# A cross-attention block on one core: another written order of the same operations, and earlier output stores

## The chip, the cores and the metric

The kernel runs on one core of a Trainium2 chip, in float32. The metric is the device time of one execution in microseconds; the median of three runs counts. The names are those of the profile: PE is TensorE (PEld its weight loads), DVE is VectorE, ACT is ScalarE, POOL is GpSimd, SP is SyncE, which issues all the DMAs here.

## The reference

One transformer block with cross-attention, four sequences of 256 tokens against 512 context rows, width 512, 16 heads of 32, an MLP of 2048:

```python
B, LQ, LK, D, H, HD, INNER = 4, 256, 512, 512, 16, 32, 2048
q = (layer_norm(x, ln1) @ q_w + q_b) -> heads
k, v = (ctx @ k_w + k_b), (ctx @ v_w + v_b) -> heads
attn = softmax(q @ k.T / sqrt(HD))
hidden = (attn @ v) @ cproj_w + cproj_b + x
y = gelu(layer_norm(hidden, ln2) @ fc_w + fc_b, approximate=True)
out = hidden + y @ proj_w + proj_b
```

## The kernel before, in words

The tokens are worked on in two groups, g = 0 and 1, each through the same stages. Context and tokens are loaded in quarters (`cq`), transposed on PE (`turn_c`, from an identity matrix, into the bank `ps_c`) and copied to SBUF (`c`). Then come the value, key and query projections (`v`, `k`, `q`), the attention units, the output projection (`o`), the second layer norm (`y`), the MLP's first matrix (`fc`) and its second (`proj`, whose products are called `pd`).

Each projection multiplies 2x2 blocks by seven products in place of eight (Strassen's scheme in Winograd's form; the two MLP matrices use it twice, 49 products for each half of `fc` and for each group of `proj`). That leaves less work to PE, and gives the other engines many elementwise sums: of weights (`vws`, `kws`, `fw`, `pw`), of operands (`y0i`, `z1t`, `z1i`) and of results. The function `quad` emits the seven products `P1` to `P7` of one block into PSUM banks `X`, `Y` and `W`, and behind each the sums that take it out (`t1`, `c11`, `c22` and so on). `P1` can be issued in two halves (`a`, `b`). `grown` runs `quad` seven times for the outer level. In the very last block, `pd14`, the product `P4` goes to a bank of its own, and the DVE sum `oz` takes it straight to the output tile. `P4`'s operand is `z1i4_4`, a sum of 1024 columns, which on POOL goes in two halves.

An attention unit is named by group, batch pair and head (`s113`, `av123`): `s` are the scores, in 32-row tiles of PE; then a multiplication by the mask, a maximum, a subtraction (`less`) and an exponential, spread over POOL, DVE and ACT; `ss` are the sums of the exponentials; `av` multiplies them with the values, in 32-column tiles of PE.

What sets the order is a string, `PROGRAM`. It holds every operation's name once, some with a letter for the engine (`:V` DVE, `:A` ACT, `:G` POOL); `Order.run` reads it and the operations are emitted in that order, so each engine, and SP for the DMAs, works through its own operations as the string has them. A waiting instruction holds up everything behind it on its engine. A second string, `PLACES`, gives each buffer its slot in SBUF or its bank in PSUM, so which earlier buffer has to be finished with first. In the trace a tile carries the name of one buffer of its slot, which is why a later product can show an operand under an earlier name.

`proj.ending` runs behind the outer products whose results are final. It transposes the finished column blocks (`tr`, on DVE), adds the residual (`out`, on DVE or POOL) and stores the result in 32-column pieces (`so`). For group 1 and the first half of the rows (I = 0) this happens twice, for L = 0 behind `pd12` or for L = 1 behind `pd13`; behind the last outer product, `pd14`, the remaining quarter is turned on PE (`turn_o`), the residual is added (`ot`), and the stores `st1`, `st00` and `st01` end the kernel.

Of the kernel before, what the change touches and what calls it, by code (L numbers as in the profile page):

```python
# [16 lines left out]
P = 128  # L17
# [109 lines left out]
v0_0_t2:V fw0_00_0 xt0_6 c0_30:A v0_1_P6 c0t4:V fw0_00_1 v0_0_P2 kws2:G fw0i1_1:G v0_1_t2:V v0_0_c11 fw0i1_2:V v0_0_P5
v0_1_P2 fw0i1_3:V fw0i1_4:V rows8 rows2 fw0_11_1 v0_1_P5 v0_1_t3:A fw0_10_1 fw0s3:V rows3 rows5 mk~1 fw0i4_1:G
fw0i7_3:V v0_0_t3:A rows1 fw0i7_1:G xt0_4 v0_1_c11 kw01 vws4:V fw0_11_0 fw0i7_2:V xt0_2 stats_x0_30 qw10 fw0i7_4:G
stats_x0_20 k0_0_P7 fw1_11_1 cols fw0_01_0 cols~1 xt0_3 aggr_x0_20 fw0s1:V fw0s2:V xt0_0 qw11 xt0_1 k0_1_P2 fw0i5_1:G  # L130
fw0_01_1 k0_0_P2 stats_x0_21 k0_1_t1:A vws3:G k0_1_P6 k0_1_t2:A fw0i4_2:G xt0_7 fcd0_1_True aggr_x0_21 stats_x0_00
stats_x0_01 k0_1_c11 fw0i4_4:V fw0i5_2:G fw0i5_4:G stats_x0_11 v0_0_P3 aggr_x0_30 k0_0_t1:A fw1_01_1 stats_x0_10
aggr_x0_10 k0_0_P6 fw0i5_3:V aggr_x0_11 aggr_x0_00 fw0i6_1:G fw1_00_1 aggr_x0_01 k0_1_P5 kws4:G v0_0_c12:A eps_x0_0
k0_0_t2:A k0_1_t3:A fw0i6_2:V k0_0_P5 pow_x0_0 fw1_00_0 stats_x0_31 fcd0_7_True nb_x0_0 k0_0_t3:A eps_x0_1 fw1_11_0
fw0i6_3:V fcd0_5_False k0_1_P7 fcd0_7_False pow_x0_1 qw00 norm_x0_01:A k0_1_P3 fw0i2_1:V cb1_03 nb_x0_1 fcd0_5_True
fw1_01_0 norm_x0_10:A fcd0_6_False v0_1_P3 k0_0_c22 qw01 fw0i6_4:G fw0i2_3:G eps_x0_2 norm_x0_11:A v0_1_c12:A
aggr_x0_31 norm_x0_00:V k0_0_c11 turn_x0_00 turn_x0_20 pow_x0_2 fw0i4_3:V k0_1_c12:A k0_1_c22 qws1:V fw1i1_1:V
fcd0_6_True nb_x0_2 fw0i2_2:G fw0i2_4:G fw0s4:V k0_0_P3 x0_20:A eps_x0_3 pow_x0_3 x0_00:V xt1_2 fw1i1_3:G cb1_01
fw1_10_1 nb_x0_3 norm_x0_31:V qws2:V norm_x0_20:A fw1i2_1:G fw0i3_3:V k0_0_c12:A fw1i1_2:V k0_1_P4 cb1_12 fw1i4_1:G
fw1i4_2:V turn_x0_30 fcd0_3_False turn_x0_10 fw1i2_2:V vd0_0_11 cb1_10 x0_10:A x0_30:A k0_0_P4 norm_x0_30:A q0_0_P1  # L140
norm_x0_21:A fw1i1_4:V k0_0_c21 fcd1_1_True q0_0_t1:A fw1i2_3:V k0_1_c21 q0_0_P2 q0_0_c11 fw1_10_0 fw1i2_4:G
turn_x0_01 x0_01:A fw1i4_4:G turn_x0_11 turn_x0_21 fcd1_2_True kd0_0_22 x0_11:V turn_x0_31 x0_31:A x0_21:A x0t1:V
x0t2:V q0_1_P1 q0_1_P2 s000 fw0i3_1:G qws3:V q0_0_P6 q0_0_t2:A ev000_11 x0t3:V fw0i3_2:G x0t4:V q0_1_t1:A fw1s1:V
fw1s2:V ev000_00 fw0i3_4:G fw1i4_3:G fcd1_4_True stats_x1_10 fw1i5_1:G fw1i5_2:G ev000_10 ev000_31 ev000_21 fw1s4:V
fw1i3_1:G q0_0_P7 q0_0_P5 q0_0_t3:A q0_0_c22 cb1_11 cb1_00 q0_1_P6 ev000_30 fw1i3_3:G cb1_02 kd0_0_11 q0_0_P4 ev000_01
kd0_0_21 fw1i3_2:G q0_1_t2:A q0_1_P5 mx000_0 ev000_20 mx000_1 q0_0_c21 mt000 q0_1_c11 mc000_3 fcd0_3_True xt1_3
fw1i5_4:G mc000_2 mc000_1 fold000 stats_x1_11 aggr_x1_10 fw1i3_4:G cT1_00 fcd1_5_False kd0_1_21 fcd1_6_False
aggr_x1_11 s020 ev020_00 ev020_10 q0_1_P7 qws4:G ev020_11 ev020_01 eps_x1_1 fcd0_2_True fw1s3:G q0_0_P3 ev020_30
fw1i6_1:V v0_0_P7 cb1_13 pow_x1_1 ev020_31 mx020_0 fcd1_3_False ev020_20 ev020_21 q0_0_c12:A md000 mx020_1 fw1i5_3:G
fw1i7_3:G mt020 nb_x1_1 cT1_01 fw1i7_1:G fw1i7_2:G q0_1_t3:A mc020_3 mc020_1 mc020_2 s002 fcd1_3_True cb1_32 ev002_11  # L150
ev002_31 fold020 fw1i6_3:G ev002_10 ev002_30 cT1_11 q0_1_P3 cT1_10 norm_x1_11:A fcd1_7_False fw1i6_2:G ev002_21
v0_1_P7 v0_0_c22 fw1i7_4:G ev002_20 ev002_01 ev002_00 mm000 md020 fw1i6_4:G fcd1_5_True q0_1_c12:V s022 ev022_11
ev022_01 ev022_00 v0_0_P4 ev022_10 cb1_33 q0_1_c22 ev022_20 ev022_30 ev022_21 q0_1_P4 c1t1:G ev022_31 s010 v0_1_c22
# [1354 lines left out]
```

## Time and profile before

| | |
|---|---|
| three runs, us | 652.28 (median), 652.1, 653.53 |
| the profiled execution, us | 652.72 |
| its span | 650.9 us |
| PE busy | 643.7 us, 99% of the span |
| DVE, ACT, POOL busy | 574.4, 346.0, 424.3 us |
| share of the chain that ended last, by PE | 88% |
| mean DMA rate | 222 GB/s |

The span runs from the first to the last instruction of the profiled execution; the 1.8 us between it and the execution's time lie outside the trace. A group row of the profile gives line, engine, operation, output and inputs, count, then busy us, mean ns of one, and the idle time just ahead of them with what ended it.

### The profile page before, as it was taken

To read this page: it belongs to the slowest core of one execution; us is meant where nothing else is said; L and a number is where in the kernel's file an instruction comes from. 1 tells how busy PE (TensorE), PEld (TensorE's weight loads), DVE (VectorE), ACT (ScalarE), POOL (GpSimd) and SP (SyncE) were. 2 spreads that over 40 slices of the span, in tenths; PEclk is the share of its full clock that TensorE was granted. 3 is DMA by queue.
4 is the path that set the end of the run, shared out by engine and by line. 5 is a ranking of instruction groups with operands and counts; after the bars stand their busy time and mean duration, and the time that the engine had idled before them with its cause. 6 is when DMAs were issued, how large, how long until landed. Compare 5 with 4: busy or idle time off the path is not lost.

```text
span 650.9 us, 11260 instructions
## 1 busy us (share of the span) xinstructions
PE 643.7 (99%) x3793; PEld 486.1 (75%) x3793; DVE 574.4 (88%) x970; ACT 346.0 (53%) x710; POOL 424.3 (65%) x377
## 2 busy tenths in 40 slices
PE   9999999999999999999999999999999999999997
PEld 7755464577445776777778888888888888888887
DVE  3998899999999999999999999999867778897684
ACT  2154689899999989976775547120220133621000
POOL 2573998888887996698959455222674536717563
PEclk9999999999999999999999999999999999999999
DMA  8999897778545459976768587979979598568855
GB/s 281 287 371 311 263 248 238 266 194 157 188 162 185 150 176 293 307 249 206 230 212 275 176 289 228 331 258 148 260 210 203 180 213 201 158 153 255 178 109 101
DMA packets 206585, 144.83 MB, mean 222 GB/s; under 512 B 117008, under 2 KB 166976, under 8 KB 206528
## 3 DMA queue, kind: packets, MB, share of 16 engines
q1 hardware_dynamic: 206528, 144.11, 77.7%
q8 instruction: 30, 0.49, 0.3%
q14 instruction: 27, 0.22, 0.1%
HBM read 104.10 MB, written 39.98 MB: 221 GB/s over the span
## 4 chain that ended last, share of the span: by engine, by line
PE 88%; DVE 6%; ACT 2%; DMA 2%; issue 1%; SPq 0%; DVEq 0%; ACTq 0%
PE pd_X L633 15%; PE fc_X L633 15%; PE fc_W L633 7%; PE pd_W L633 7%; PE av L633 6%; PE k_X L633 4%; PE s L633 4%; PE v_X L633 4%; PE pd_Y L633 4%; PE fc_Y L633 3%; PE o_X L633 3%; PE q_X L633 2%; PE k_W L633 2%; PE o_W L633 2%; PE v_W L633 2%; DVE mx L1032 2%
## 5 line engine op out<-in xcount | busy, mean ns | idle before, releaser
L613 ACT ACTIVATE pr<-s,cols 128x256 f32<-128x256 f32 x256 | 103.4, 484 | 11.6 <-PE s L633 7.4
L1056 POOL TENSOR_TENSOR pr<-pr,mm 128x512 f32<-128x512 f32 x76 | 100.1, 1348 | 2.8 <-DMA mm<-md 2.5
L1032 DVE TRANSPOSE_TENSOR_REDUCE mx<-pr 128x32 f32<-128x1024 f32 x64 | 76.7, 1218 | 2.1 <-ACT pr L613 1.9
L1236 ACT ACTIVATE h<-h,cols 128x256 f32<-128x256 f32 x128 | 54.7, 500 | 43.3 <-DVE h L624 24.5
L1059 ACT ACTIVATE pr<-pr 128x1024 f32<-128x1024 f32 x64 | 66.8, 1067 | 16.9 <-DVE pr L1052 8.3
L624 DVE TENSOR_TENSOR h<-fc_X,h 128x512 f32<-128x512 f32 x80 | 52.8, 675 | 7.2 <-PE fc_X L633 6.2
L624 DVE TENSOR_TENSOR h<-fc_W,h 128x512 f32<-128x512 f32 x48 | 31.8, 676 | 2.7 <-PE fc_W L633 2.3
L1052 DVE TENSOR_TENSOR pr<-pr,mm 128x1024 f32<-128x1024 f32 x26 | 33.4, 1303 | 0.0
L624 POOL TENSOR_TENSOR ss<-pr 128x512 f32<-128x512 f32 x19 | 25.6, 1357 | 10.8 <-ACT pr L1059 8.1
L1039 ACT COPY mx<-mx 32x64 f32<-32x64 f32 x96 | 23.3, 243 | 12.5 <-issue 5.8
L633 PE MATMUL pd_W<-z0i,pl 128*128 128x256 f32 x104 | 24.4, 379 | 0.0
L605 ACT ACTIVATE e<-pd_X,cols 128x256 f32<-128x256 f32 x4 | 1.9, 469 | 39.5 <-PE pd_X L633 26.0
L633 PEld LDWEIGHTS pd_W<-z0i,pl 128*128 128x128 f32 x104 | 19.8, 190 | 2.7
L624 DVE TENSOR_TENSOR po<-pd_X,po 128x256 f32<-128x256 f32 x24 | 9.9, 418 | 12.5 <-PE pd_X L633 12.5
L633 PE MATMUL pd_X<-z1i,pl 128*128 128x256 f32 x88 | 20.8, 379 | 0.0
L1040 DVE TENSOR_REDUCE mx<-mx 32x32 f32<-32x256 f32 x32 | 18.5, 579 | 2.6 <-ACT mx L1039 2.1
L624 POOL TENSOR_TENSOR tq<-tq,rq 128x512 f32<-128x512 f32 x8 | 10.1, 1266 | 16.2 <-DMA rq<-hd 11.6
L633 PE MATMUL fc_W<-y1i,fl 128*128 128x256 f32 x76 | 19.2, 380 | 0.0
L633 PE MATMUL pd_X<-z0i,pl 128*128 128x256 f32 x80 | 18.9, 379 | 0.0
L633 PEld LDWEIGHTS pd_X<-z1i,pl 128*128 128x128 f32 x88 | 16.7, 190 | 2.3
L624 POOL TENSOR_TENSOR h<-h,e 128x512 f32<-128x512 f32 x11 | 14.6, 1348 | 5.7 <-DVE e L624 5.7
L624 DVE TENSOR_TENSOR h<-fc_Y,h 128x512 f32<-128x512 f32 x24 | 16.1, 673 | 2.6 <-PE fc_Y L633 2.5
(603 smaller groups left out, 1865.8 us busy)
## 6 DMA issues: line engine op xcount, KB each, us to landing
mm<-md SPq DMA_DIRECT2D x32, 512.0 KB, 4.2
pl<-prd SPq DMA_DIRECT2D x56, 256.0 KB, 4.1
fl<-fcd SPq DMA_DIRECT2D x40, 256.0 KB, 3.5
fw<-in_L_xattn_fc_w_dram SPq DMA_DIRECT2D x16, 256.0 KB, 4.6
pw<-in_L_xattn_proj_w_dram SPq DMA_DIRECT2D x32, 128.0 KB, 3.0
hid<-in_x_dram SPq DMA_DIRECT2D x8, 512.0 KB, 3.9
hd<-hid SPq DMA_DIRECT2D x8, 512.0 KB, 5.7
fcd<-fw0i SPq DMA_DIRECT2D x7, 512.0 KB, 3.0
```

The costliest lines, as they stand in the source:

```text
L605: nc.scalar.activation(to(), of_(), AF.Identity, bias=bias(), scale=1.0)
L613: lambda e: nc.scalar.activation(to(), of_(), AF.Identity, bias=bias(), scale=1.0))
L624: E[e].tensor_tensor(to(), in0(), in1(), op)
L633: nc.tensor.matmul(o(), l(), r(), start=first, stop=True, skip_group_check=True)
L1032: T.op(f"mx{u}_{h}", [("DVE", 1.126)], [(pr[h], None)], [(mx, [h])], lambda e, h=h: nc.vector.tensor_reduce(tile_of(mx)[:, 0:64].rearrange ...
L1039: lambda e, a=a: nc.scalar.copy(tile_of(mx)[0:32, 64 + 64 * a : 128 + 64 * a], tile_of(mx)[32 * a : 32 * a + 32, 64:128]))
L1040: T.op(f"fold{u}", [("DVE", 0.38)], [(mx, [2, 3, 4, 5])], [(mx, [6])], lambda e: nc.vector.tensor_reduce(tile_of(mx)[0:32, 320:352], tile_ ...
L1052: nc.vector.tensor_tensor(p_, p_, m_[:, None, :].to_broadcast([P, 2, 512]), ALU.subtract)
L1056: E[e].tensor_tensor(p_, p_, m_, ALU.subtract)
L1059: lambda e, h=h: nc.scalar.activation(tile_of(pr[h]), tile_of(pr[h]), AF.Exp), table="exp")
L1236: lambda e, f=f, b=b, c=c: nc.scalar.activation(at(h[f][b], c), at(h[f][b], c), AF.Gelu_apprx_tanh, bias=col(c_fcb + f * 4 + c), scale=1.0 ...
```

## The change

Three things change. `PROGRAM` is replaced by another order of the same operations: 2999 names in place of 2991, with other engine letters at 123 elementwise operations. `PLACES` is replaced by another assignment of slots and banks. And in `proj.ending`, for group 1 and I = 0, each half of a column block is stored as soon as its own `out` is done, in sixteen stores of 64 KB in place of eight of 128 KB. The number of matmuls and of elementwise operations stays the same. Behind the tables all lines move down by two.

```diff
 PROGRAM = """
-cq0_00_0 vw00 cq0_00_1 turn_c0_10_0 turn_c0_00_0 c0_00_0:V c0_10_0:A small v0_0_P1a cq0_01_1 cq0_01_0 turn_c0_10_1
+cq0_00_0 turn_c0_10_0 turn_c0_00_0 vw00 c0_10_0:A c0_00_0:V small v0_0_P1a cq0_00_1 cq0_01_0 turn_c0_00_1 c0_00_1:V
...
 PLACES = """
...
-                if last:
+                if g == 1 and I == 0:
+                    for a in range(4):
+                        store(f"so{g}_{c}{a}_{L}", None, None, [(tq[c], [2 * L, 2 * L + 1])],
+                              lambda c=c, a=a: o_[512 * L : 512 * L + 512, c * P + 32 * a : c * P + 32 * a + 32].rearrange("(t i) j -> i t j", i=32),
+                              lambda c=c, a=a: tile_of(tq[c])[32 * a : 32 * a + 32, 512 * L : 512 * L + 512].rearrange("p (t j) -> p t j", j=32), 0.165)
+                elif last:
                     for a in range(4):
                         store(f"so{g}_{c}{a}", None, None, [(tq[c], [2 * x + y for x in part for y in range(2)])], lambda c=c, a=a: view[c][1](o_, a),
...
```

Three places of the new order follow. In a row stand the line, the operation, output and inputs with the number of the buffer behind the name, the shape, and how many such instructions follow each other.

At the start of the kernel, PE's instructions from the first value product on, in before. `v0_0_X` and `v0_1_X` are the banks of the first two value products, and the `ps_c` rows are transposes of the context quarters:

```order
L633 MATMUL v0_0_X_222<-vw00_206,c0_00_215 128x256 x2
L721 MATMUL ps_c0_10_1_228<-ident_64,cq0_00_204 128x128 x2
L721 MATMUL ps_c0_00_1_231<-ident_64,cq0_00_204 128x128 x2
L633 MATMUL v0_0_X_222<-vw00_206,c0_00_215 128x256 x2
L721 MATMUL ps_c0_11_247<-ident_64,cq0_01_225 128x128 x4
L721 MATMUL ps_c0_01_255<-ident_64,cq0_01_225 128x128 x4
L633 MATMUL v0_1_X_264<-vw00_206,c0_00_215 128x256 x4
```

The same stretch of PE in after:

```order
L635 MATMUL v0_0_X_221<-vw00_212,c0_00_214 128x256 x2
L723 MATMUL ps_c0_00_1_227<-ident_64,cq0_00_204 128x128 x2
L723 MATMUL ps_c0_10_1_231<-ident_64,cq0_00_204 128x128 x2
L635 MATMUL v0_0_X_221<-vw00_212,c0_00_214 128x256 x2
L635 MATMUL v0_1_X_239<-vw00_212,c0_00_214 128x256 x2
L723 MATMUL ps_c0_01_244<-ident_64,cq0_01_225 128x128 x4
L723 MATMUL ps_c0_11_252<-ident_64,cq0_01_225 128x128 x4
L635 MATMUL v0_1_X_239<-vw00_212,c0_00_214 128x256 x2
```

The first half of the second product now stands ahead of the transposes of the second quarter (`cq0_01`), the other half behind them.

In the attention units' last part, PE between two products of `fc015`, in before (`av123` and `s113` are two units' tiled matmuls, the others full-array products):

```order
L633 MATMUL fc015_X_3426<-y0t1_3084,fl015_0_3372 128x256 x2
L633 MATMUL av123_3432<-ss123_3366,ones_89 32x256 x4
L633 MATMUL av123_3432<-pr123_0_3135,vws1_297 32x256 x2
L633 MATMUL av123_3432<-pr123_1_3126,vws1_297 32x256 x2
L633 MATMUL av123_3432<-pr123_0_3135,vws1_297 32x256 x2
L633 MATMUL av123_3432<-pr123_1_3126,vws1_297 32x256 x2
L633 MATMUL fc015_Y_3453<-y0t1_3084,fl015_0_3372 128x256 x2
L633 MATMUL fc015_X_3426<-y0i5_3368,xn_x1_11_859 128x256 x2
L633 MATMUL s113_0_3464<-q1_1_12_2165,kw00_239 128x256
```

The same place in after:

```order
L635 MATMUL fc015_Y_3429<-y0t1_3017,v1_1_12_1657 128x256 x2
L635 MATMUL fc015_X_3408<-y0i5_3367,k1_0_11_998 128x256 x2
L635 MATMUL av123_3441<-ss123_3383,ones_89 32x256 x4
L635 MATMUL av123_3441<-pr123_0_3117,kw11_350 32x256 x2
L635 MATMUL av123_3441<-pr123_1_3148,kw11_350 32x256 x2
L635 MATMUL av123_3441<-pr123_0_3117,kw11_350 32x256 x2
L635 MATMUL av123_3441<-pr123_1_3148,kw11_350 32x256 x2
L635 MATMUL s113_0_3461<-kw11_350,xt0_5_444 128x256
```

`fc015_Y` (its `P2`) and the next `fc015_X` (its `P6`) no longer stand between the two units: `s113` follows `av123` directly, so one change from full-array to tiled matmuls falls away.

POOL's last operations in before (`tq` are the `out` sums, `po` the sums of finished blocks, `z1i4_4` the operand of the last product):

```order
L622 TENSOR_TENSOR z1i2_4_5733<-h1_30_4856,z1i2_2_5640 128x512 x2
L622 TENSOR_TENSOR z1i4_3_5755<-z1t4_3_5653,z1t4_1_5599 128x512 x2
L624 TENSOR_TENSOR po1_0_5205<-po1_0_5205,e1_5390 128x256
L624 TENSOR_TENSOR po1_1_5311<-po1_1_5311,e1_5390 128x256 x2
L624 TENSOR_TENSOR tq1_1_5775<-tq1_1_5775,rq1_1_5628 128x512
L622 TENSOR_TENSOR z1i4_4_5816<-z1t4_2_5729,z1i4_2_5694 128x512 x2
```

The same in after:

```order
L624 TENSOR_TENSOR z1t4_3_5714<-h1_31_4870,z1t2_3_5413 128x512 x2
L626 TENSOR_TENSOR tq1_0_5695<-tq1_0_5695,rq1_0_5311 128x512
L624 TENSOR_TENSOR z1i4_2_5731<-z1t4_3_5714,z1i4_1_5726 128x512 x2
L624 TENSOR_TENSOR z1i4_3_5781<-z1t4_3_5714,z1t4_1_5698 128x512 x2
L626 TENSOR_TENSOR po1_1_5354<-po1_1_5354,e1_5411 128x256
L626 TENSOR_TENSOR tq1_0_5695<-tq1_0_5695,rq1_0_5311 128x512
L626 TENSOR_TENSOR tq1_1_5648<-tq1_1_5648,rq1_1_5433 128x512
L624 TENSOR_TENSOR z1i4_4_5832<-z1t4_2_5611,z1i4_2_5731 128x512 x2
```

`out1_00` and `out1_10` (the two `tq` rows ahead of the last) now stand right ahead of `z1i4_4`; before, one such sum stood there, and it was another, `out1_11`.

More of the change, by code (lines that the diff above doesn't have):

```diff
@@ L127 @@
[L127 to L131, printed above, removed]
```

663 lines of the change are left out of this document (335 added, 328 removed).

## The prediction

> **What bounds the kernel now.** I read the page's engine shares first, then the chain that ended last, then a table of stretches, then the tensor engine's list of waits. Of the page these are the span, the busy times and the chain's shares by engine:
>
> ```profile
> span 650.9 us, 11260 instructions
> PE 643.7 (99%) x3793; PEld 486.1 (75%) x3793; DVE 574.4 (88%) x970; ACT 346.0 (53%) x710; POOL 424.3 (65%) x377
> PE 88%; DVE 6%; ACT 2%; DMA 2%; issue 1%; SPq 0%; DVEq 0%; ACTq 0%
> ```
>
> PE is busy for 643.7 of 650.9 us and carries 88% of the chain, and it has the same 3793 matmuls to do after the change. So the change can help only where PE waits, where PE changes between kinds of matmul, and at the two ends; it can hurt wherever another engine comes to be late for PE. The stretches below (length, then busy us and count for PE, its weight loads, DVE, ACT, POOL, then granted clock, DMA share, GB/s) show where that could be:
>
> ```profile
> core 0: us, PE busy (x) PEld busy (x) DVE busy (x) ACT busy (x) POOL busy (x), PEclk, DMA share, GB/s
> 0.00:25.00 25.00, 23.41 (x130) 19.19 (x131) 13.45 (x22) 4.37 (x7) 9.84 (x16) 1.00 0.88 268
> 25.00:50.00 25.00, 25.00 (x77) 13.45 (x76) 23.07 (x49) 11.03 (x17) 17.66 (x20) 1.00 1.06 351
> 50.00:75.00 25.00, 25.00 (x104) 12.50 (x103) 20.92 (x30) 12.99 (x26) 14.77 (x16) 1.00 0.97 298
> 75.00:100.00 25.00, 25.00 (x149) 14.43 (x148) 23.58 (x39) 21.48 (x52) 23.00 (x23) 1.00 0.98 253
> 425.00:450.00 25.00, 25.00 (x118) 22.00 (x117) 23.39 (x29) 3.51 (x5) 7.15 (x4) 1.00 0.84 224
> 625.00:651.00 26.00, 22.65 (x117) 19.94 (x115) 15.60 (x33) 0.00 (x0) 11.66 (x11) 1.00 0.53 97
> ```
>
> The clock is full everywhere, so it drops out. The first and last stretches are the only ones where PE is short of its 25 us by more than a little. The list of PE's waits (engine, line waited for, total us, times, longest) says how much could be won between them:
>
> ```profile
> PE ps_c L721 <- DMA cq<-in_ctx_dram: 0.6, 1, 0.6
> PE av L633 <- DVE ss L624: 0.5, 1, 0.5
> PE q_X L633 <- ACT q L605: 0.5, 1, 0.5
> PE o_W L633 <- DVE hid L624: 0.4, 1, 0.4
> PE q_X L633 <- ACT k L605: 0.4, 1, 0.4
> PE s L633 <- DVE q L624: 0.3, 1, 0.3
> PE fc_X L633 <- ACT xn_x L600: 0.2, 1, 0.2
> ```
>
> The first row lies at the start (below). The other six sum to 2.3 us in the whole middle of the kernel. That is small: nearly 3000 operations are reordered, and at most 2.3 us of waiting is there to be removed.
>
> **The start.** PE's first groups (start, length, the waiting time before it in brackets):
>
> ```profile
> 6.50 1.03 PE L633 MATMUL v_X<-vw,c 128*128 128x256 f32 x4
> 8.13 1.06 PE L721 MATMUL ps_c<-ident,cq 128*128 128x128 f32 x8 [0.60 <-DMA cq<-in_ctx_dram]
> 9.03 1.89 PE L633 MATMUL v_X<-vw,c 128*128 128x256 f32 x8
> 10.76 1.04 PE L721 MATMUL ps_c<-ident,cq 128*128 128x128 f32 x8
> ```
>
> Eight records of a value product take 10.76−9.03 = 1.73 us, so one is 0.216 us, and the group at 6.50 is over at 6.50+4×0.216 = 7.36. (The list's 0.60 reckons with a modelled end; start to start the gap is 8.13−7.36 = 0.77.) The change puts the first half of the next value product, four such records or 0.86 us, ahead of the two transposes that wait for that load. It needs only a quarter that has already been turned, and both copies of it, now on DVE, are out by about the time at which it starts. 0.86 covers 0.77, so I take the whole −0.77. Bounds: 0, if the later loads set the pace of the next products in any case, to −0.77. I take the upper end because the next transposes, at 10.76, start without any wait behind the product ahead of them; how much earlier than that their load lands, these rows don't say.
>
> **Changes of matmul kind.** The scores and the attention-times-value products use 32-row or 32-column tiles of PE. The order now joins some of these blocks: 36 separate visits stand between the full-array products, where 39 stood. One visit in before, with the products around it:
>
> ```profile
> 115.24 1.88 PE L633 MATMUL k_W<-c1t,kws 128*128 128x512 f32 x4
> 116.96 1.88 PE L633 MATMUL k_Y<-c,xt 128*128 128x512 f32 x4
> 118.77 0.64 PE L633 MATMUL av<-ss,ones 128*32 128x256 f32 x8
> 119.22 1.05 PE L633 MATMUL av<-pr,xt 128*32 128x256 f32 x16
> 120.20 1.98 PE L633 MATMUL k_X<-c,k 128*128 128x512 f32 x4
> 122.02 1.88 PE L633 MATMUL k_W<-c1t,vw 128*128 128x512 f32 x4
> ```
>
> A full product takes 116.96−115.24 = 1.72. k_Y is thus over at 118.68, and the visit starts at 118.77: 0.09 to enter. The product behind the visit takes 122.02−120.20 = 1.82: 0.10 more than the plain one. A visit costs 0.19 by these, and three fewer give −0.57, taken as −0.6. I do not count the cost of leaving the tiled matmuls, since where two blocks are joined they change between rows and columns inside the block instead. Bounds: 0, if PE had to wait there for an operand in any case, to −0.9 with some 0.1 each for leaving too.
>
> **The waits in the middle.** The same PE work stands ahead of every one of the six waiting products as before, so no new cover is put there, and what they wait for goes through the same engines. The one that the change touches is `av012`: the subtraction ahead of its exponentials goes from POOL to DVE, but its two sums of exponentials go from DVE to POOL. I take −0.3 for all six together. Bounds: −2.3 (all gone) to several us more (the second rival).
>
> **Engines.** 65 of the elementwise operations go from POOL to DVE (35 of 256 columns, 12 of 512, 18 of 1024), 60 from DVE to POOL (26, 19, 15), 20 from ACT to DVE and 18 from DVE to ACT. The rows that price them (DVE for 512, 1024, 256 columns, then POOL's two halves of a 1024-wide one with operands from elsewhere or from POOL itself):
>
> ```profile
> L624 DVE TENSOR_TENSOR h<-fc_X,h 128x512 f32<-128x512 f32 x80 | 52.8, 675 | 7.2 <-PE fc_X L633 6.2
> L624 DVE TENSOR_TENSOR z1t<-h,z1t 128x1024 f32<-128x1024 f32 x7 | 8.7, 1257 | 0.0
> L624 DVE TENSOR_TENSOR po<-pd_X,po 128x256 f32<-128x256 f32 x24 | 9.9, 418 | 12.5 <-PE pd_X L633 12.5
> L622 POOL TENSOR_TENSOR z1i<-h,z1i 128x512 f32<-128x512 f32 x8 | 12.6, 1586 | 6.9 <-DVE z1i L624 5.9 <-DMA out_dram<-tq 0.8 <-ACT h L1236 0.2
> L622 POOL TENSOR_TENSOR z1i<-z1t,z1i 128x512 f32<-128x512 f32 x10 | 12.4, 1269 | 1.4 <-issue 1.4
> ```
>
> Net, DVE gets 9×0.418 − 7×0.675 + 3×1.257 from POOL and two more of 0.675 from ACT: 3.76 − 4.73 + 3.77 + 1.35 = +4.2 us on 574.4. I cost it at nothing. Its cover is DVE's idle time: 1.93 + 4.08 + 1.42 = 7.4 us in the three stretches from 25 to 100 us, by the table, and the lead that the vector engine's results have over the product that reads them. The uneven part is early. Of the sums of MLP weights a net twelve 256-wide ones, one of 1024 and two of 512 come to DVE before about 110 us, and one of 512 leaves: 12×0.418 + 1.257 + 0.675 = 6.9 us, just under those 7.4. If that cover fails, it is the second rival. From about 376 us on PE does not wait at all (the stretch from 425 shows 25.00 of 25.00 with DVE at 23.39), and the order of products against their operands is no tighter there than before, so I count nothing.
>
> **The end.** The last PE groups, POOL's and DVE's last operations, and the stores (the last row: count, issue time min/median/max, first and last start):
>
> ```profile
> 643.02 1.89 PE L633 MATMUL pd_X<-z1t,pl 128*128 128x256 f32 x8
> 644.75 1.12 PE L1321 MATMUL ps_o<-ident,po 128*128 128x128 f32 x8
> 645.70 1.95 PE L633 MATMUL pd_V<-pl,z1i 128*128 128x128 f32 x16
> 641.13 1.27 POOL L624 TENSOR_TENSOR tq<-tq,rq 128x512 f32<-128x512 f32 x1 [4.63 <-issue]
> 642.36 2.50 POOL L622 TENSOR_TENSOR z1i<-z1t,z1i 128x512 f32<-128x512 f32 x2
> 647.69 0.42 DVE L624 TENSOR_TENSOR ot<-pd_V,ot 128x256 f32<-128x256 f32 x1 [0.89 <-PE pd_V L633]
> L593 SPq DMA_DIRECT2D out_dram<-tq x32: 315/506/1105, 525.2 to 644.1; - x32
> ```
>
> The last product, at 645.70, reads the sum `z1i4_4`, which POOL ends at 644.86: 0.84 early. In the new order POOL does `out1_10` right ahead of it, and `out1_10` needs results of the last but one block, `pd12`. From the end of that block's fourth product to the last product PE has three products and four transposes: 3×1.73 + 0.95 = 6.1 us. On the other side stand one sum (0.42), a transpose of about the same length, another sum and transpose, then 1.27 and 2.50 on POOL: 4×0.42 + 3.77 = 5.45, and by estimate a tenth for each of four or five handovers between engines (the nearest row is the 0.09 that PE took to enter a visit): 5.8 to 6.0. The 0.84 of slack shrinks to 0.1 or 0.3, and I take +0.1 since so little can be gone. Bounds: 0 to +0.8, the latter if POOL works at its slower row (1.586 for each of the three in place of 1.26, which makes the chain about 6.9).
>
> The eight last stores become sixteen of half the size. Ten go out behind the last two sums, and at 506 ns each SP is through with them at about the last product's start; the final store waits for DVE's 647.69 in any case. I take 0, hidden beside the last product and the sum behind it; uncovered it is up to 3×0.506 = +1.5. [...]
>
> **The sum.** −0.77 − 0.6 − 0.3 + 0.1 = −1.6 us, on a profiled execution of 652.72, which is 0.44 above the median of 652.28 and 1.8 longer than its span. Against the median: 650.7.
>
> **Rivals.** First, no change that can be told: the first and second terms hold, but waits grow elsewhere by about as much. The clearest place is POOL before the last product: at 1.586 for each operation the chain is 6.9 against PE's 6.1, +0.8 in place of +0.1, which gives −0.9 or 651.4. For it speaks that both paces stand in the profile for the same kind of operation, and that POOL gets one more late output sum; against it, that the very operations in question show the quick pace (the rows at 641.13 and 642.36). With new waits of under a microsecond at some of the attention products it is 651.4 to 652.3. [...]
>
> Second, slower: the 6.9 us of early weight sums are not absorbed by DVE. Its 7.4 us of idle are then not free time but waits for PE and for the loads (the DMA share is 0.97 to 1.06 there), and the lateness is carried on into the attention products, of which PE reads every result. Against it: those sums are wanted only by the MLP hundreds of microseconds later, and each is a word in a written order that can stand in a gap. Wholly unabsorbed it gives 652.3 − 1.6 + 6.9 = 657.6; half, 654.1. It decides from 1.6 + 1.3 = 2.9 us unabsorbed.
>
> Third, more than forecast: the 2.3 us of mid waits all vanish, because results come earlier through the new choice of engines: 650.7 − 2.0 = 648.7. For it speaks that fewer products now have their last operand's producer written close ahead of them (146 before, 129 now, with less than nothing to spare by the rows' durations); against it, the six places are the same.
>
> **How the numbers follow.** The forecast itself (650 to 651) has 0.38, the third 0.10, the first 0.32, the second 0.20. Measurements of this kernel can tell about 0.2%, 1.3 us, from no change; the first rival's time lies within that (over 651.0), the forecast and the third below it, the second above 653.6. So faster 0.48, same 0.32, slower 0.20. The range reaches down to 648.4 (the third, a little below it) and up to 654.6 (somewhat over half of the second), and leaves out some 0.06 below and 0.1 above.
>
> **What would show it.** The start: the wait for `cq` gone, and the 10.76 group 0.8 us earlier. The visits: 36, each still 0.2. The middle: PE's list of waits between 1 and 3 us. DVE: about 578 us busy, PE full from 25 to 75 us. The end: `z1i4_4` over within 0.3 us of the last product's start, and every half store landed before the final store. I am wrong if PE shows several short waits between 75 and 376 us that sum to over 2 us (the second rival), or if the loads after the first five land later than before.

## The result, and the profile after

The changed kernel is slower. Twenty executions of it have a median of 659.6 us (657.0 to 662.82), twenty of the kernel before on the same chip 657.41; the ratio of the comparison is 1.0078, with a 95% interval of 1.0056 to 1.0099. The forecast was 650.7 and a gain. One thing is needed to read these numbers: the kernel before has groups of times (651 to 655, 656 to 661 and 662 to 665 us), the ratio leaves the uppermost out, and the three times ahead of the prediction all came from the lowest; the first experiment tells why.

Three facts ahead of the prediction are to be put right: the inputs are eight sequences of 256 tokens, each against 256 context rows, and what is spread over POOL and DVE in an attention unit is the subtraction of the maximum, `less` (the `pr<-pr,mm` rows), while the mask is a bias that is added as the scores are copied out of PSUM. And 163 elementwise operations have another engine letter, not 123: the 65, 60, 20 and 18 of the prediction. None of the three enters the sum.

The page of the changed kernel, in the same three parts:

```profile
span 658.8 us, 11274 instructions
PE 647.1 (98%) x3793; PEld 487.1 (74%) x3793; DVE 579.9 (88%) x977; ACT 344.9 (52%) x708; POOL 411.4 (62%) x369
PE 66%; DVE 14%; ACT 7%; DMA 3%; POOL 3%; issue 3%; SPq 2%; DVEq 0%; ACTq 0%; POOLq 0%
```

PE has the same 3793 matmuls, but only 66% of the chain that ended last, where it had 88; DVE has 14 in place of 6. The span is 7.9 us longer: PE is idle for 4.5 us more, and busy for 3.4 us more with the same matmuls. Of these 3.4, some are slower first products, and some may be short waits, since the profile models the ends of matmuls (eight records that follow each other every 1.73 us are 1.89 us long in it). The stretches say where, first the changed kernel's, then two of the kernel before that were not shown:

```profile
core 0: us, PE busy (x) PEld busy (x) DVE busy (x) ACT busy (x) POOL busy (x), PEclk, DMA share, GB/s
0.00:25.00 25.00, 23.98 (x127) 19.25 (x128) 12.55 (x23) 6.33 (x11) 5.39 (x12) 1.00 0.81 247
50.00:75.00 25.00, 25.00 (x101) 12.26 (x100) 23.27 (x36) 11.88 (x25) 10.72 (x13) 1.00 1.01 301
200.00:225.00 25.00, 23.05 (x214) 15.64 (x207) 24.43 (x39) 22.66 (x51) 20.50 (x14) 1.00 0.33 115
375.00:400.00 25.00, 23.48 (x122) 18.67 (x121) 24.31 (x32) 13.80 (x34) 15.38 (x12) 1.00 0.52 174
```

```profile
200.00:225.00 25.00, 24.68 (x231) 16.95 (x228) 24.69 (x41) 23.86 (x55) 22.53 (x17) 1.00 0.52 171
375.00:400.00 25.00, 25.00 (x117) 21.84 (x116) 24.86 (x41) 12.76 (x31) 14.62 (x12) 1.00 0.76 245
```

From 25 to 75 us, where more weight sums came to DVE, PE is full. The largest losses lie at 200 to 225 and at 375 to 400 us, 1.6 and 1.5 us, where DVE is no busier than before. (Another 1.5 us is lost from 475 to 525 us, in the trace with late loads.) PE's list of waits in the changed kernel (engine, line waited for, total, times, longest):

```profile
PE s L635 <- DVE v L626: 1.9, 1, 1.9
PE fc_X L635 <- DMA fl<-fcd: 1.0, 2, 0.8
PE o_X L635 <- DVE a1t L626: 1.0, 1, 1.0
...
PE av L635 <- ACT pr L1061: 0.5, 1, 0.5
PE fc_W L635 <- DMA fl<-in_L_xattn_fc_w_dram: 0.5, 1, 0.5
PE fc_W L635 <- DVE h L626: 0.5, 1, 0.5
```

Between the start and the end there are seven waits of 0.5 us or more (1.9, 1.0, 0.8 and four of 0.5), where the kernel before had two. Most are of two kinds, late DVE results and loads of MLP weights (`fl`). The longest is `s110` at 216 us. DVE's rows just ahead of it, then POOL's, then PE's (start, length, and the wait in brackets):

```profile
210.11 0.40 DVE L626 TENSOR_TENSOR pw0i<-pw0i,pw 128x256 f32<-128x256 f32 x1
210.44 1.49 DVE L626 TENSOR_TENSOR pw0i<-pw 128x256 f32<-128x256 f32 x1
211.85 1.50 DVE L626 TENSOR_TENSOR pw0i<-pw,pw0i 128x256 f32<-128x256 f32 x1
213.27 2.29 DVE L1054 TENSOR_TENSOR pr<-pr,mm 128x1024 f32<-128x1024 f32 x1
215.49 0.68 DVE L626 TENSOR_TENSOR v<-q_Y,v 128x512 f32<-128x512 f32 x1
```

```profile
210.16 1.49 POOL L624 TENSOR_TENSOR a0t<-att,a0t 128x512 f32<-128x512 f32 x1 [0.36 <-POOL a0t L624]
211.80 1.27 POOL L624 TENSOR_TENSOR a0t<-att,a0t 128x512 f32<-128x512 f32 x1 [0.15 <-ACT att L615]
213.03 3.67 POOL L1058 TENSOR_TENSOR pr<-pr,mm 128x512 f32<-128x512 f32 x2
```

```profile
216.22 1.15 PE L635 MATMUL s<-v,v 32*128 32x256 f32 x16 [1.95 <-DVE v L626]
```

The two rows of 1.49 and 1.50 are the weight sums `pw0i1_3` and `pw0i1_4`, which the change took from POOL to DVE. Sums of 256 columns were priced at 0.418, and the one at 210.11 does take 0.40. Those two, and the subtraction behind them, each start 0.05 to 0.28 us behind the start of a POOL sum and end behind its end, the two sums by 0.28 us (211.93 and 213.35 against 211.65 and 213.07), the subtraction by 1.08: each of the two sums takes 1.08 us more than its 0.42. The row at 215.49, which reads PSUM, has its ordinary 0.68; it is `q1_1_c11`, it is only late, and PE waits for it. The subtraction was stretched in the kernel before too (2.29 us at 211.02); the two sums are new there, and their 3 us are more than the wait. The second place, at 376 us, is a 1024-wide sum (`xb1_0`) that starts 0.3 behind the same sum for another block on POOL (`xb1_1`), and takes 3.39 us:

```profile
376.10 3.39 DVE L1429 TENSOR_TENSOR hid<-hid,cb 128x1024 f32<-128x1024 f32 x1
```

```profile
375.82 2.59 POOL L1429 TENSOR_TENSOR hid<-hid,cb 128x1024 f32<-128x1024 f32 x1 [1.73 <-DVE h L626]
```

```profile
380.14 1.13 PE L635 MATMUL fc_W<-y0i,qws 128*128 128x256 f32 x4 [0.51 <-DVE h L626]
...
384.01 2.21 PE L635 MATMUL o_X<-qws,a1t 128*128 128x256 f32 x9 [1.00 <-DVE a1t L626]
```

Both PE groups wait for DVE results queued behind it.

### The profile page after: what moved, and what is told of

Its sections match the earlier page's. It is cut to its first block, busy times and chain, and to the rows that moved or that the text cites. A ratio compares the mean times of both kernels' runs of the same rounds, so it can differ in the third digit from the quotient of the medians.

```text
span 658.8 us, 11274 instructions
## 1 busy us (share of the span) xinstructions
PE 647.1 (98%) x3793; PEld 487.1 (74%) x3793; DVE 579.9 (88%) x977; ACT 344.9 (52%) x708; POOL 411.4 (62%) x369
## 4 chain that ended last, share of the span: by engine, by line
PE 66%; DVE 14%; ACT 7%; DMA 3%; POOL 3%; issue 3%; SPq 2%; DVEq 0%; ACTq 0%; POOLq 0%
PE pd_X L635 14%; PE fc_X L635 10%; PE pd_W L635 7%; PE fc_W L635 5%; PE av L635 4%; PE pd_Y L635 3%; ACT pr L615 3%; PE k_X L635 3%; DVE mx L1034 3%; PE q_X L635 3%; DVE h L626 3%; PE fc_Y L635 2%; PE s L635 2%; PE v_X L635 2%; POOL pr L1058 2%
## 5 line engine op out<-in xcount | busy, mean ns | idle before, releaser
L1058 POOL TENSOR_TENSOR pr<-pr,mm 128x512 f32<-128x512 f32 x74 | 96.5, 1332 | 6.5 <-DMA mm<-md 6.5
L626 POOL TENSOR_TENSOR ss<-pr 128x512 f32<-128x512 f32 x24 | 30.8, 1295 | 14.3 <-ACT pr L1061 11.9
L624 POOL TENSOR_TENSOR z1t<-h,z1t 128x512 f32<-128x512 f32 x10 | 15.9, 1605 | 16.3 <-PE pd_X L635 15.9
L624 POOL TENSOR_TENSOR z0i<-z0t,z0i 128x512 f32<-128x512 f32 x10 | 13.4, 1357 | 19.5 <-issue 9.9
L626 POOL TENSOR_TENSOR tq<-tq,rq 128x512 f32<-128x512 f32 x11 | 14.9, 1367 | 11.7 <-DMA fl<-fcd 5.6
L635 PE MATMUL fc_X<-y1i,fl 128*128 128x256 f32 x80 | 20.4, 380 | 0.8 <-DMA fl<-fcd 0.8
L626 DVE TENSOR_TENSOR po<-pd_W,po 128x256 f32<-128x256 f32 x24 | 9.9, 418 | 10.4 <-PE pd_W L635 10.2
L635 PE MATMUL pd_X<-z1i,pl 128*128 128x256 f32 x80 | 19.0, 380 | 0.0
L635 PEld LDWEIGHTS fc_X<-y1i,fl 128*128 128x128 f32 x80 | 15.1, 190 | 3.2 <-DVE h L626 1.2
L635 PE MATMUL av<-pr,ones 128*32 128x256 f32 x256 | 16.9, 382 | 0.5 <-ACT pr L1061 0.5
```

The source lines that it names most:

```text
L624: nc.gpsimd.tensor_tensor(to()[:, ts(k, 512)], in0()[:, ts(k, 512)], in1()[:, ts(k, 512)], op)
L626: E[e].tensor_tensor(to(), in0(), in1(), op)
L635: nc.tensor.matmul(o(), l(), r(), start=first, stop=True, skip_group_check=True)
L1058: E[e].tensor_tensor(p_, p_, m_, ALU.subtract)
```

## The experiments

The theory after this reading is that DVE's sums of two SBUF operands and POOL's sums take turns, as under a lock: whichever starts second is held until the other is done. The rivals were plain overload of DVE, and the loads.

**The kernel before, once more.**

> The kernel before, unchanged, for a second trace. Its twenty times lie in two groups, 652 to 654 and 657 to 665 us. If waits of PE on late DVE and POOL results make the difference (the theory of the shared lock), a slower run shows the same products with more or longer waits between 130 and 390 us, at DVE sums that are stretched from 0.42 to about 1.5 us while POOL is in a sum. If loads make it (the rival), the waits stand on DMAs. In either case the start should show whether PE runs its first products at 0.22 or at 0.43 us a record.

659.05 us, an execution of the upper groups. Up to 226 us it is the same as the first, within 1.3 us. Then `a0t4`, a 1024-wide sum, which took DVE 1.69 us in the first trace, takes 5.41. The row of the first trace, then this one's:

```profile
226.85 1.69 DVE L624 TENSOR_TENSOR a0t<-att,a0t 128x1024 f32<-128x1024 f32 x1
```

```profile
226.81 5.41 DVE L624 TENSOR_TENSOR a0t<-att,a0t 128x1024 f32<-128x1024 f32 x1
```

```profile
224.94 9.62 POOL L1056 TENSOR_TENSOR pr<-pr,mm 128x512 f32<-128x512 f32 x7
```

```profile
236.04 6.72 PE L633 MATMUL o_W<-vws,a0t 128*128 128x256 f32 x16 [4.10 <-DVE hid L624]
```

```profile
234.00:236.00 2.00, 0.00 (x0) 0.00 (x0) 2.00 (x4) 1.35 (x4) 2.00 (x3) 0.83 0.23 68
236.00:238.00 2.00, 1.96 (x5) 1.60 (x6) 2.00 (x4) 0.11 (x1) 1.02 (x1) 0.50 0.54 190
```

POOL has seven sums on end there. In the first trace DVE came in between the second and the third; here it was passed over at three such borders. PE then waits 4.1 us, and when it goes on the granted clock is 0.50 for 6.8 us, and the two products of 1.73 each take 6.56 us together. The wait (4.2 us, start to start) and the slow products (3.1) cost 7.3 us together, where the first trace lost 0.5; the span is 6.4 us longer. Over all 115 executions of the kernel before that were timed beside the experiments, the mean granted clock parts the groups: 0.999 to 1.000 in the 57 between 650.8 and 654.8 us, 0.995 to 0.997 in the 38 from 656.5 to 661.5, 0.992 in the 20 from 662.2 to 665.4. A clock of 0.50 for 6.8 us, as in this trace, makes 0.995. Of the load rival nothing is seen. PE's first product also ran slowly here, as in the changed kernel (below).

**The changed kernel, once more.**

> The changed kernel, unchanged, for a second trace. Theory of the lock: the waits at s110 (2.0 us), o1_0_P2, fc013_P4 and o1_0_P6 (2.5 us together) come again within 0.5 us each, since the order fixes which DVE sum meets which POOL sum. Rival, chance in the loads: they fall elsewhere. The three waits for weight loads between 493 and 502 us (2.1 us) come again if the order of the loads makes them.

657.1 us. The waits at `s110` (2.01) and at `o1_0_P2`, `fc013_P4` and `o1_0_P6` (0.61, 0.77, 1.17) come again to the hundredth: the order fixes these meetings. The three waits for weight loads do not come at all. So the changed kernel has a fixed loss on DVE and a chance loss on loads.

**The sums by themselves.**

> Only elementwise sums on DVE and POOL, none of the block's computation: each engine alone, then both together with DVE's operands both in SBUF (256 and 1024 columns), with one in PSUM (512), and mixed. Theory of the lock: DVE's 256-column sum takes 0.42 us alone and on average well over 0.8 beside POOL's 1.27, the two taking turns, while the sums with an operand in PSUM stay at 0.67 with POOL's pace unchanged. [...] Second rival (none): 0.42 throughout.

This run holds such sums and little else, none of the block's computation. The groups that ran together, in pairs of DVE and POOL (256 columns of SBUF beside POOL, 1024 of SBUF, then 512 with one operand in PSUM); the last row is the PSUM sum with POOL idle:

```profile
L58 DVE TENSOR_TENSOR vo<-va,vb 128x256 f32<-128x256 f32 x40 | 39.6, 990 | 1.7 <-POOL go L44 0.4
L56 POOL TENSOR_TENSOR go<-ga,gb 128x512 f32<-128x512 f32 x24 | 31.9, 1330 | 1.9
L63 DVE TENSOR_TENSOR vo<-va,vb 128x1024 f32<-128x1024 f32 x20 | 42.4, 2119 | 1.0 <-POOL go L44 0.4
L61 POOL TENSOR_TENSOR go<-ga,gb 128x512 f32<-128x512 f32 x24 | 47.7, 1986 | 1.9
L68 DVE TENSOR_TENSOR vo<-bank,vb 128x512 f32<-128x512 f32 x40 | 27.6, 691 | 1.7 <-POOL go L44 0.4
L66 POOL TENSOR_TENSOR go<-ga,gb 128x512 f32<-128x512 f32 x24 | 30.3, 1264 | 1.9
L51 DVE TENSOR_TENSOR vo<-bank,vb 128x512 f32<-128x512 f32 x12 | 8.3, 691 | 0.4
```

The means mix two values, since POOL's group is over before DVE's, or the other way about. While both run, every 256-wide DVE sum takes 1.37 us (0.42 alone), one for each POOL sum; every 1024-wide one 2.17 (1.23 alone), and POOL's 2.12 in place of 1.26. The PSUM sums take 0.691 beside POOL and alone, and POOL's stay at 1.264. This is taking turns: the theory's numbers, and not 0.42 throughout. The turns overlap a little, though: the pairs follow each other every 1.40 and 2.20 us, where the two instructions alone would sum to 1.68 and 2.49, an overlap of 0.3 us.

**Four operations moved out of the meetings.**

```diff
-ev120_11 o0_1_P1 pw0i1_3:V mc122_3 mc102_1 pw0i1_4:V a0t1:G less100_0:V ab0_111 q1_1_c11 mc102_3
+ev120_11 o0_1_P1 mc122_3 mc102_1 a0t1:G less100_0:V ab0_111 q1_1_c11 pw0i1_3:V pw0i1_4:V mc102_3
...
-a1t1:V pw1i6_1:V hid1_1
+a1t1:V hid1_1
...
-xb1_1:G xb1_0:V fc013_c22
+xb1_1:G xb1_0:G fc013_c22
...
-a1t2:V gelu0_202
+a1t2:V pw1i6_1:V gelu0_202
```

> The changed kernel with four operations moved: the weight sums pw0i1_3 and pw0i1_4 behind q1_1_c11, pw1i6_1 behind a1t2, and xb1_0 to POOL. Theory of the lock (DVE sums of two SBUF operands are held up by POOL's at these places, and PE's products wait for what is queued behind them): the waits at s110 (2.0 us) and at o1_0_P2, fc013_P4 and o1_0_P6 (2.5 us) fall to under 1 us together, the kernel gains 3 to 4 us against the changed one, some 656 us. Rival (DVE simply has too much to do there): the waits come back at the next products, the time stays at 659 to 660. Rival (the loads): no change either, with the waits on DMAs.

656.22 us (654.12 to 660.45 in 12), 3.4 less than the changed kernel's median, as the theory had it. (Here and below, a run's 12 executions are set against the changed kernel's 20, which were not timed beside them; the 95% interval of this difference, by resampling, is 1.9 to 5.3.) The wait at `s110` is gone, and `o1_0_P2` and `fc013_P4` no longer wait. What was said of the rest is half a miss: 1.03 us come back at `o0_0_P6`, behind the moved sums, and 1.59 at `o1_0_P6`, which now waits for `xb1_0` on POOL. DVE has as much work as before the edit but for one sum, so plain overload did not make the waits that went.

**The sum that DVE is passed over at, on POOL.**

```diff
-mc130_2 a0t4:V ev112_00
+mc130_2 a0t4:G ev112_00
```

> The kernel before with one letter changed: the operand sum a0t4 (1024 columns, two operands in SBUF) goes to POOL. In the slower trace of before DVE was held at this sum for 5.4 us, over three POOL sums on end, PE waited 4.2 us for what stood behind it and then ran at half clock for 6 us. Theory of the lock: the group of times from 657 to 665 us goes, nearly all runs lie within 652 to 655 us, and the trace shows no wait over 1 us at o0_0_P7. Rival (the two groups come from loads or from the clock by itself): the spread stays, 652 to 665, whatever engine does the sum. Second rival: POOL's 2.5 us more make its subtractions late and the attention products wait for them, all runs at 654 to 656.

All 12 executions lie between 650.68 and 653.7, median 653.07, while of 23 of the kernel before beside them 10 lie between 651.46 and 653.32 and 13 between 656.49 and 664.03. The ratio is 0.9968 (0.9939 to 0.9997). One letter takes the upper groups away, and the second rival's later attention products do not show. The mean granted clock is 0.999 to 1.000 in all 12. This version beats the kernel before by 0.3% on the comparison, and by more where the upper groups count; its median is also 6.5 us below the changed kernel's, which was not timed beside it. The group at 662 to 665 was not traced: its clock of 0.992 would by estimate be some 10 us at 0.50 (twice 0.008 of 662 us), but how many borders are passed over there is open.

**One sum alone, in the kernel before.**

```diff
-vu013 pw0i1_3:G ows3:V
+vu013 ows3:V
...
-mm100 less100_0:V
+mm100 pw0i1_3:V less100_0:V
```

> The kernel before with one weight sum, pw0i1_3, moved from POOL to DVE and put right ahead of less100_0, where the changed order has it. By the prediction's price it costs DVE 0.42 us and the wait at s110 grows from 0.34 to at most 0.8. Theory of the lock: the sum takes 1.4 to 1.5 us there since POOL is in a sum of its own, and the wait at s110 grows to between 1.3 and 2 us.

A miss in place, not in kind. The moved sum takes 0.41, and `s110` waits 0.55. But without it POOL starts its next sum (`xb0_0`) at 201.25 in place of 203.41, and that meets two other DVE sums (0.68 and 0.41 in before, where they began just ahead of POOL's sums):

```profile
201.51 2.88 DVE L624 TENSOR_TENSOR vws<-v,ow 128x512 f32<-128x512 f32 x1
...
204.91 1.99 DVE L624 TENSOR_TENSOR pw0i<-pw 128x256 f32<-128x256 f32 x1
```

```profile
PE s L633 <- DVE att L624: 2.1, 1, 2.1
```

PE waits 2.1 us inside the scores behind them, and its next products run at half clock for 3.4 us: 656.94. What an operation leaves behind on its old engine can cost more than its place on the new one.

**The two waits that were left.**

```diff
-o0_1_P1 pw0i1_3:V mc122_3 mc102_1 pw0i1_4:V a0t1:G
+o0_1_P1 mc122_3 mc102_1 a0t1:G
...
-o0_0_t1 ow01
+o0_0_t1 pw0i1_3:V pw0i1_4:V ow01
...
-xb1_1:G xb1_0:V fc013_c22
+xb1_0:G xb1_1:G fc013_c22
...
-ab1_111 o1_1_t1 pd01_P2 hid1_3 a1t2:V gelu0_202
+ab1_111 a1t2:V o1_1_t1 pd01_P2 hid1_3 pw1i6_1:V gelu0_202
```

(`pw1i6_1` is taken from its old place too.)

> The changed kernel as in the run with four operations moved, with two waits that were left or made there attended to: pw0i1_3 and pw0i1_4 behind o0_0_t1 too, xb1_0 ahead of xb1_1 on POOL, a1t2 ahead of o1_1_t1. Theory of the lock with order: the waits at o0_0_P6 (1.0 us) and o1_0_P6 (1.6 us) go, 2 to 2.5 us less than the 656.2 of that run, some 654. Rival (lateness is only pushed on): the waits come back behind them, 656 to 657.

657.64 us (655.99 to 661.02), 2.0 below the changed kernel (0.8 to 3.5): the rival was right. The waits come back one product later: 1.54 at `o0_1_P6`, 1.25 at `s132`, 1.41 around `av133`, and 1.05 for a weight load. DVE is busy 24.4 of 25 us there in the changed kernel, and the sums that stepped aside were late for the next product.

**The store split, by itself.** From here on the base is the kernel before with `a0t4` on POOL, whose times are narrow. The edit is that of `proj.ending` in the change, with the halves' names written into the order behind their sums.

```diff
-rq1_10 z1t4_2:V
+rq1_10 so1_00_1 so1_01_1 so1_02_1 so1_03_1 z1t4_2:V
...
-pd17_12~1:G tr1_12
+pd17_12~1:G so1_10_0 so1_11_0 so1_12_0 so1_13_0 tr1_12
```

> The kernel before with a0t4 on POOL (653.07 us, span 651.3) and, of the change, only the split stores: each half of the last column blocks is stored as soon as its own sum is done, sixteen stores of half the size. The prediction's step: hidden, 0 (bounds 0 to +1.5). From the start of the last product to the end of the span 5.2 us as before. [...]

From the last product's start to the end of the span it is 5.22 us (5.21 without): hidden, as forecast. Yet the median is 654.32, 1.25 more, for a reason of my own making: I had put four stores ahead of a weight load on SP, and PE waits for that load 18 us ahead of the end:

```profile
633.66 1.96 PE L634 MATMUL pd_W<-z1i,pl 128*128 128x256 f32 x8 [1.55 <-DMA pl<-in_L_xattn_proj_w_dram]
```

The change has them elsewhere in SP's order, and no such wait.

**The start, by itself.**

```diff
-c0_00_1:A v0_0_t1:V turn_c0_11 vw10 mk turn_c0_01 c0_01:A vw11 v0_1_P1a v0_1_P1b
+c0_00_1:A v0_1_P1a v0_0_t1:V turn_c0_11 vw10 mk turn_c0_01 c0_01:A vw11 v0_1_P1b
```

> The kernel before with a0t4 on POOL and, of the change, only the first half of the second value product moved ahead of the transposes that wait for the second context quarter. The prediction's step: -0.77 us where PE runs its first product at full clock. Rival, from four traces in which PE ran its first product at about 0.35 us a record in place of 0.24: the clock's rise, not the load, sets the start in most executions, and the gain is 0 to -0.8, -0.4 in the mean; the wait at turn_c0_11 (1.03 us in the trace with a0t4 on POOL) shrinks by up to 0.86 in either case.

652.93 us against 653.07: nothing that can be told. The wait for `cq` goes, as forecast, but 0.4 us come back at a sum on POOL (`vws`) that a later value product reads.

**Two ACT results earlier.**

```diff
-vu011 ev033_21 ev033_31 fold031 r003 att003 mt013 q1_0_t2:A
+vu011 q1_0_t2:A ev033_21 ev033_31 fold031 r003 att003 mt013
...
-ev122_21 ev122_11 md033 att011
+ev122_21 md033 att011
...
-vu031 ev122_00 q1_1_t3:A q1_0_P4
+vu031 q1_1_t3:A ev122_11 ev122_00 q1_0_P4
```

> The kernel before with a0t4 on POOL and two evacuations of query products moved ahead of two attention evacuations on ACT (q1_0_t2 ahead of ev033_21, q1_1_t3 ahead of ev122_11), where PE waits 0.53 and 0.63 us. If a wait that stands in the order of one engine can be removed without another in its place, the gain is 1.0 us (0.15%). Rival, after the run with later sums in which each wait came back at the next products: below 0.4 us, or a loss where the shifted DVE sums meet POOL's in another way.

652.79 us against 653.07 (one of the 12 executions took 1124 us at a mean granted clock of 0.56; it has no trace). The two waits go from PE's list; 0.5 us come back in `s120`. The gain of 0.3 lies within what the rival allows and can't be told from none (interval −0.4 to 1.2).

**Two sums back on POOL, in the changed kernel.**

```diff
-o0_1_P1 pw0i1_3:V mc122_3 mc102_1 pw0i1_4:V a0t1:G
+o0_1_P1 mc122_3 mc102_1 a0t1:G
...
-a0t2:G ab0_100
+a0t2:G pw0i1_3:G pw0i1_4:G ab0_100
```

> The changed kernel with one part of it undone: the two weight sums pw0i1_3 and pw0i1_4 back on POOL, behind a0t2, and nothing else. In two traces of the changed kernel they take DVE 1.49 us each and PE waits 2.0 us at s110. By the prediction's price they were 0.84 us of that, and 1.2 us of the wait stays. Theory of the lock: the wait at s110 falls under 0.5 us, and 1.5 to 2 us are gained against the changed kernel (659.6 in its runs, 657 to 663): about 657.5. Rival (only pushed on): the wait comes back at o0_0_P6 or s112, no gain.

658.38 us (656.25 to 662.67), 1.2 less than the changed kernel, which the noise does not rule out as nothing (−0.9 to 3.3). The trace decides: `s110` no longer waits at all, so the two sums made the whole 2.0 us and not 0.84 of it; but 1.03 us come back at `o0_0_P5` and 0.65 at `s132`, and in the traced execution some 2 us each in `av133` and at a weight load, each with 3.4 us at half clock behind it, which the run cannot put down to its edit.

**The other half of the four.** The edit is the last three pieces of the run with four operations moved.

> The changed kernel with the other half of the run with four operations moved: pw1i6_1 behind a1t2 and xb1_0 on POOL, nothing else. In the changed kernel xb1_0 takes DVE 3.39 us beside POOL's xb1_1, and PE waits 0.6, 0.8 and 1.2 us at o1_0_P2, fc013_P4 and o1_0_P6. Theory of the lock: the first two go and the third is at most 1.6, a gain of about 1 us; with the 2.0 at s110 still there some 658 to 658.5. Rival: the gain of 3.4 us of that run came from here alone.

657.87 us (655.53 to 661.72), 1.7 less than the changed kernel (−0.1 to 3.3). `s110` waits 2.01 again, and the waits at `o1_0_P2` and `fc013_P4` are gone. So in the traces each half takes away its own place; the times (1.2, 1.7, and 3.4 for both) agree with a sum of the two but are too noisy to show it. This trace also shows what a late load does:

```profile
501.12 1.95 PE L635 MATMUL fc_X<-y1i,fl 128*128 128x256 f32 x4 [2.00 <-DMA fl<-fcd]
```

```profile
502.00:504.00 2.00, 2.00 (x6) 1.64 (x5) 0.69 (x1) 0.00 (x0) 1.44 (x2) 0.50 1.09 183
```

2.0 us of waiting for `fl116_2`, and again half the clock behind it, for 3.4 us: 3.9 us in all, start to start.

**The loads, in the changed kernel.** In its order 47 of the MLP weight loads leave SP less than 8 us ahead of the product that reads them, against 29 before. Five loads that are wanted later go behind the late one.

```diff
-pd04_P7 rq0_22 fl105_3 pl04_3
+pd04_P7 rq0_22 pl04_3
...
-fc106_P6 fl116_2 fc116_P6
+fc106_P6 fl116_2 fl105_3 fl117_0 fl116_3 fl112_3 rq0_11 fc116_P6
```

> The changed kernel with five loads that are wanted 10 to 40 us later (fl105_3, fl117_0, fl116_3, fl112_3, rq0_11) moved behind fl116_2 in SP's order, nothing else. In four of six traces of the changed kernel and its variants PE waits 1 to 4.3 us for fl116_2 and its neighbours between 492 and 507 us, in two not at all. If the tighter order of the loads makes these waits: they go, the upper end of the times (657 to 663) comes down by 2 us and more, the median by 1 to 2, and the spread is under 4 us. Rival (the loads are late for another cause than their place, the bandwidth): the waits stay, at other loads; no gain.

658.04 us (656.83 to 660.7): 1.6 less (0.6 to 2.8), a spread of 3.9, and in the one trace no wait on a load. The same loads in another order do not come late there, which speaks for the place in SP's order and not the bandwidth. (The trace still shows 2.01 at `s110` and 2.7 around `av133`. Behind the wait at `s110` the clock was 0.50 for 3.4 us here, which it was not in the changed kernel's two traces; the last section sets the three beside each other.)

**Both together.**

> The same five loads moved in the kernel with four operations moved (656.2 us, 654.1 to 660.5), so both causes attended to. If the two are separate and add up: 654 to 655 us, a spread under 3 us, PE waiting only for late DVE and ACT results. Rival: 656 as before.

655.5 us (654.12 to 657.49), 4.1 below the changed kernel (3.2 to 5.7), a spread of 3.4, and only late DVE, ACT and POOL results in PE's list. Alone the two gave 3.4 and 1.6; whether they add up in full can't be told, since the step from the run with four operations moved to this one is 0.7 with an interval of −0.8 to 2.5. Against the kernel before the ratio is 0.9999 (0.9964 to 1.0034); its lowest group, at 652.3 beside this run, is still 3 us faster.

## Why the prediction was wrong, by its own steps

I sum PE's starts against its products' own lengths in each trace, by part: excess up to 25 us, the changes of matmul kind, all other waits, and the end. The first trace of before has 0.95, 11.06, 4.16 and 5.21 us (last product's start to the end), the changed kernel's second trace 1.57, 10.56, 8.45 and 5.22; its first trace has 11.43 of waits, the difference being mostly loads. The waits at `s110` (2.0) and at `o1_0` and `fc013` (2.5) are together as much as the 4.3 by which 8.45 exceeds 4.16; all other gains and losses cancel.

The start: forecast −0.77, measured +0.6. The wait for `cq` went, as forecast. But the first trace of before had a lucky start:

```profile
4.49 0.68 PE L645 MATMUL first<-warm 128*64 128x64 f32 x8
5.09 1.13 PE L633 MATMUL v_X<-vw,c 128*128 128x256 f32 x4
```

```profile
4.78 1.12 PE L647 MATMUL first<-warm 128*64 128x64 f32 x8
5.83 1.45 PE L635 MATMUL v_X<-vw,c 128*128 128x256 f32 x4
...
7.79 1.89 PE L635 MATMUL v_X<-vw,c 128*128 128x256 f32 x8
```

The same eight small matmuls take 0.68 in before (the upper pair) and 1.12 in after. In the second trace of before they take 1.04 from start to next start, as in after, and its wait for `cq` is gone too. So the step's row was one of two possible starts. The granted clock column, at 1.00 in these first microseconds, does not show what parts the two, but the changes of clock kept with the traces do: the first rise to full clock stands at 4.12 us in the first trace of before, ahead of these eight matmuls, and behind their start at 6.63 in the second, and at 6.52 and 6.87 in the changed kernel's.

The visits: forecast −0.6, measured about −0.5. That step held, three visits at close to the row's 0.19.

The end: forecast +0.1, measured 0. The chain through `out1_10` came out as drawn, at POOL's quick pace:

```profile
649.17 1.27 POOL L626 TENSOR_TENSOR tq<-tq,rq 128x512 f32<-128x512 f32 x1 [2.00 <-DVE tq L1350]
650.40 2.50 POOL L624 TENSOR_TENSOR z1i<-z1t,z1i 128x512 f32<-128x512 f32 x2
```

`z1i4_4` is over at 652.90 and the last product starts at 653.59, 0.69 later, no wait. The first rival, with its slow POOL pace here, is out.

The middle: forecast −0.3, measured +4.3 in the trace without late loads and +7.3 in the one with them. This step failed, and with it the one on engines, "I cost it at nothing". The sum was made of durations of operations that ran without a meeting (0.418, 0.675, 1.257), and DVE's busy time did come out close to it, at 579.9 against 578.6. What cost time were not the 4.2 us but where they lay: two weight sums of 0.42 that took 1.49 each ahead of a result PE needs, and one sum of 3.39. The prediction had the two POOL rows of 1269 and 1586 ns in hand and read them as a slower pace of POOL at the end; it did not ask what DVE pays. In the trace of before 31 DVE operations already stood out by 0.15 us or more over the middle of their form, 16.6 us in all, and it would have been enough to list them with POOL's row beside each.

The second rival, slower, got the sign and the size (654 to 658) but not the mechanism: it put the loss at 25 to 100 us, at the early weight sums, and there the cover held (25.00 of 25.00 up to 75 us, 24.87 in the next 25). The sign that was named for it, short waits between 75 and 376 us of over 2 us in all, did come, from the two places above.

Loads were not priced at all beyond the start: SP's order for the MLP weights had become tighter (47 loads against 29), and the run with moved loads puts that at 1.6 us.

Last, the base: 652.28 was the median of three executions of the lowest group. That a sum may be passed over by POOL and cost 6.4 us is in no single trace of the low group, but the 1.69 us of `a0t4`, in place of some 1.2, stood there.

Settled by runs are: the lock (the sums alone), its price at two places of the changed kernel (the traces of the four sums and of each half), that the loads' order matters, the hidden stores, and that `a0t4` makes the kernel before's upper groups. Not settled are the 3 us that still part the version with both remedies from the lowest group of before; they are waits of 0.3 to 1.3 us on DVE and ACT results between 100 and 391 us, several of them at attention products, which no run took away one by one.

## What to carry to other kernels

Price an elementwise operation that is moved between DVE and POOL by what the other engine does at that moment: in these runs one with two SBUF operands cost its own length, or up to that and most of one of the other engine's (0.42 became 1.37 to 1.50 beside sums of 1.26), and sums with an operand in PSUM were free of it (0.691 beside POOL and alone). A sum taken off an engine let that engine's next one start earlier (at 201.25 in place of 203.41) and meet others, so a written order is moved as a whole or checked in a trace, and waits of PE of 2 to 4 us had 3.4 to 6.8 us at half clock behind them in some traces. Take more than one trace of a kernel before trusting three agreeing times: one with two groups of times needs a trace from each.

## What the runs showed of the hardware that I had not expected

DVE lost the turn several times on end: a 1.2 us sum took 5.41 us while it was passed over at three borders between POOL sums that ran one behind the other, where in the sums alone the two engines alternated strictly. And POOL did not always pay: beside a 256-wide DVE sum its 512-wide one took 1.33 us in the mean, hardly more than its 1.26.

Whether a wait cost clock as well went with where it fell. In the traces the later changes of the granted clock lie a whole multiple of 3.413 us behind the first rise: 190 of them in the first trace of before (648.53 us), 191 in the changed kernel's first (651.95), 67 in the second trace of before (228.7), 62 in the run with moved loads (211.6), 145 in the run with the other half (494.9). Where the end of the run does not cut it off, the half clock lasts 3.41 us, or twice that in the second trace of before. Cut at these multiples, a trace falls into cells. The cells in which PE stood idle for 2.0 us (the run with the other half, ahead of 501.2), 2.92 (the changed kernel, ahead of 658.46) and 3.41 (before, ahead of 652.65) were followed by 0.50; of those with 1.49 (the changed kernel at 214.7) and 1.58 (before at 645.8) neither was. The same wait of 2 us at `s110` left the clock at 1.00 in three traces, where a border between two cells fell into it (1.49, 1.32 and 1.09 us of idle in its fuller cell), and had 0.50 behind it in the run with moved loads, where it lay inside one cell. The first rise shows where the cells lie, and in the traces of the two kernels it stands anywhere from 4.12 to 6.87 us, so the same wait did not cost the same in every execution.
